# A second mixture of experts whose outputs are scattered to tokens instead of gathered by them

## The chip, the cores and the metric

The kernel runs on one NeuronCore of a Trainium2 chip. The core has a matrix engine (PE), a vector engine (DVE), a scalar engine (ACT), a general engine (POOL, also GpSimd) and a queue engine (SP); each runs its own instruction list in order, and they wait for each other through semaphores. Transfers between memory (DRAM) and the on-chip memory (SBUF) are issued from the SP, ACT or POOL queue and carried out by 16 DMA engines. PE writes its results to PSUM, eight banks that DVE and ACT read. The metric is the device time of one execution, in microseconds (us); less is better.

## The reference

The input is x of 8 sequences of 512 tokens with 128 channels, 4096 tokens in all, in f32. Two layers follow one another, each of the form x + s * silu(g), where s and g are both computed from the normalised x:

```python
xn = layernorm(x)
s = mamba_and_mlp(xn)               # layer 0: a selective scan over 512 steps, then an MLP, two rms norms
g = silu(moe0(xn))                  # 24 experts, top 2 of each token, hidden width 512
x = x + s * g
xn = layernorm(x)
s = attention(xn)                   # layer 1: 8 causal heads
g = silu(moe1(xn))                  # 128 experts, top 2, at most 32 tokens each
x = x + s * g
```

The second mixture (moe1) is where most of the change lies. Each token picks its two best experts, e1 and e2; its place in an expert is the number of earlier tokens that chose it, and second choices come behind all first choices. A choice with a place of 32 or more is dropped:

```python
buf = zeros((E * C, d)).at[idx1].add(xt * v1).at[idx2].add(xt * v2)   # E = 128, C = 32
yb = einsum('ecd,edf->ecf', buf, we)
y = (g1 * v1) * yb[idx1] + (g2 * v2) * yb[idx2]
```

g1 and g2 are the two softmax gates, divided by their sum; v1 and v2 are 1 where the choice was kept.

## The kernel before, in words

**Order.** The Python program is traced into instructions. A planner then orders each engine's list: it starts an instruction when its model says that the inputs and buffers are there, and among ready ones takes the one written earlier. So an instruction can move ahead of others written before it, but once the lists are made, every engine runs its list in order, and one that waits holds all behind it. `follows` and `keep_in_program_order` add edges that fix the order of two instructions of one engine without a wait.

**First layer.** `prepare(b)` normalises a sequence and stores it (`xn_dram`); `places0` and `routing` work out the first mixture's places. `mixture` runs its 24 experts in two passes: `expert1` gathers tokens by POOL's indirect DMAs (L128), multiplies and stores; `between` normalises the hidden rows; `expert2` (L512) gathers them, adds the output bias (L524) and multiplies (L526). The bias is added by a matmul of K = 96 in bf16: the f32 bias is split into three bf16 parts, kept one under another in `bias`, and `chosen(e, r)` picks the three rows of one expert. The recurrent model (`model`, with `front`, `scan`, `back`) is cut into 64 steps that `step()` writes between the experts, and later between the attention heads. Each batch's model result s is stored to `s_dram` (L706).

**Second layer.** `fetch(b)` (L530) loads `o`, `sb` (the stored s) and `xb`, and adds the first mixture's rows to `o` by 8 indirect DMAs (L131). `after` (L545) makes the second layer's input of them: a layernorm, silu, product with `sb` on POOL (L551) and sum (L552). `Attention.prepare` (L752) normalises, finds the top two of 128 experts and the sum of exponentials `se1`, makes the attention's input and calls `route`. `route` (L793) counts places, makes `idx1` (the slot row of each choice, or a spare row beyond the slots) and `row1` (the row of the choice in the output table), and sends each token's row to its slot by 8 scatters per batch (L833), to one table for first choices and one for second choices (`xs_dram[0]`, `xs_dram[1]`). Both tables are zeroed near the start (L272).

Batches 0 to 5 (`EARLY`) run their heads beside the model; batches 6 and 7 run them in the last stage, after the model's end. There, `weights2` (L918) makes the gate weights of all tokens in one pass, and `places` (L930) makes `live`, which is 1 for a slot that may hold a token. `slots(t)` (L956) loads 512 slots of each table and transposes them into `xsT`; `experts(e0)` (L974) multiplies eight experts' slots with their weights into one PSUM bank, DVE multiplies by `live` (L980), and the result is stored to `yb_dram` in one DMA (L981).

`finish(b)` (L983) loads the attention result and the second layer's input of a batch, gathers for each of its four token groups the two rows of `yb_dram` (L993 and L994, through the helper L128, 8 indirect DMAs for each batch), multiplies them by the two weights and adds (L995, L996), takes silu (L997), multiplies by s (L998), adds x (L999) and stores (L1000).

The last stage has 16 heads. They are written with a list of other work: `slots(0)` behind the first head, then 16 experts behind each of the next eight heads, then one `finish` behind each of the next six, and `finish(6)` and `finish(7)` behind the last.

Of the kernel before, what the change touches and what calls it, by code (L numbers as in the profile page):

```python
# [20 lines left out]
P = 128  # L21
# [12 lines left out]
S1 = E1 * C1  # L34
HEADS, DHEAD = 8, 128
# [12 lines left out]
def tile_kernel(ctx: ExitStack, tc: tile.TileContext, t: dict, out: bass.AP):  # L48
# [42 lines left out]

    xs_dram = [dram.tile([S1 + P, D], F32, name=f"xs_dram{k}") for k in range(2)]
    yb_dram = dram.tile([2 * S1, D], F32, name="yb_dram")

# [75 lines left out]
    w121 = w3.tile([P, NTT, 2], F32, name="w121")  # L170
    row1 = w3.tile([P, NTT, 2], I32, name="row1")
    idx1 = w3.tile([P, NTT, 2], I32, name="idx1")
    kp1 = w3.tile([P, NTT, 2], F32, name="kp1")
# [22 lines left out]
    bias = inv_pool.tile([3 * 32, DH + D], BF16, name="bias")  # L196
    zero = inv_pool.tile([P, L], F32, name="zero")
    G.memset(zero, 0.0)
# [72 lines left out]
    for k in range(2):  # L271
        empty = Q.dma_start(  # L272
            xs_dram[k][0:S1, :].rearrange("(p n r) d -> p n (r d)", p=P, r=L // D),
            bc(zero.unsqueeze(1), (P, S1 // L, L)),
        )
        follows(empty, kept)
# [44 lines left out]
    eb = xp.tile([3 * 32, DH + D], F32, name="eb", bufs=1)  # L321
    G.memset(eb, 0.0)
    for k in range(3):
        Q.dma_start(eb[32 * k : 32 * k + E0, 0:DH], t["eb1"])
        Q.dma_start(eb[32 * k : 32 * k + E0, DH:], t["eb2"])
    part = xp.tile([3 * 32, DH + D], BF16, name="part", bufs=1)
# [116 lines left out]
    def expert1(e, w):  # L443
# [10 lines left out]
        for c, r in enumerate(SROWS):  # L454
            ph = ps_e.tile([CP, DH], F32, name="ph", tag="pe")
            T.matmul(ph[:r], chosen(e, r), bias[:, 0:DH], start=True, stop=False)
            T.matmul(ph[:r], xT[:, c * CP : c * CP + r], we, start=False, stop=True)  # L457
            S.activation(hs[:r, c, :], ph[:r], AF.Copy, scale=wsl[:r, c, e : e + 1])
# [53 lines left out]
    def expert2(e, w):  # L512
# [4 lines left out]
        for c, r in enumerate(SROWS):  # L517
# [6 lines left out]
            T.matmul(po[:r, c, :], chosen(e, r), bias[:, DH:], start=True, stop=False)  # L524
            for f in range(NJ):
                T.matmul(po[:r, c, :], hT[:, f, :r], we[:, f, :], start=False, stop=(f == NJ - 1))  # L526
# [3 lines left out]
    def fetch(b):  # L530
# [3 lines left out]
        sb = af.tile([P, NJ, D], F32, name="sb")  # L534
        Q.dma_start(sb, rows(s_dram[b][:, :]))
# [130 lines left out]
    def back(b, yt):  # L666
# [39 lines left out]
        Q.dma_start(rows(s_dram[b][:, :]), xo)  # L706
        yield

# [36 lines left out]
    class Attention:  # L745


        def __init__(self, at, m_qk, w_vo, ps_x, ps_q, ps_s, ps_t, ps_o):
            self.at, self.m_qk, self.w_vo = at, m_qk, w_vo
            self.ps_x, self.ps_q, self.ps_s, self.ps_t, self.ps_o = ps_x, ps_q, ps_s, ps_t, ps_o  # L750

        def prepare(self, b, xb):  # L752

            at, (ps_x, px) = self.at, self.ps_x
            xn2 = at.tile([P, NJ, D], F32, name="xn2", bufs=1)
            layernorm(st, xb, xn2, NJ, eps5, "ln1")
            pt = ps_x.tile([P, L], F32, name="pt2", tag=px)
            for j in range(NJ):
                T.transpose(pt[:, j * P : (j + 1) * P], xn2[:, j, :], ident)
# [15 lines left out]

            sq = at.tile([P, NJ, D], F32, name="sq2", bufs=1)
            ss = st.tile([P, NJ], F32, name="ss2")
            for j in range(NJ):
                S.activation(sq[:, j, :], xn2[:, j, :], AF.Square, accum_out=ss[:, j : j + 1])
# [4 lines left out]
            V.tensor_tensor(sq, xn2, bc(ss.unsqueeze(2), (P, NJ, D)), ALU.mult)  # L784
# [8 lines left out]
        def route(self, b, xn2):  # L793
# [28 lines left out]
            kp = kp1[:, bs, :]  # L822
# [5 lines left out]
            for k in range(2):  # L828
                V.tensor_scalar(pos[:, :, k], pos[:, :, k], float(C1 - 1), float(k * C1), ALU.min, ALU.add)
            V.scalar_tensor_tensor(row1[:, bs, :], e12, float(2 * C1), pos, ALU.mult, ALU.add)  # L830
# [68 lines left out]
        def heads(self, b, xaT):  # L899
# [3 lines left out]
            for hd in range(HEADS):  # L903
# [9 lines left out]
                if hd == HEADS - 1:  # L913
                    Q.dma_start(rows(s1_dram[b][:, :]), s1)
                yield


    def weights2():  # L918
        V.reciprocal(se1, se1)
        V.tensor_tensor(w121, mx1[:, :, 0:2], bc(mx1[:, :, 0:1], (P, NTT, 2)), ALU.subtract)  # L920
        S.activation(w121, w121, AF.Exp)
        V.tensor_tensor(w121, w121, bc(se1.unsqueeze(2), (P, NTT, 2)), ALU.mult)
        den = r3.tile([P, NTT], F32, name="den1")
        V.tensor_tensor(den, w121[:, :, 0], w121[:, :, 1], ALU.add)
        V.tensor_scalar(den, den, EPS32, None, ALU.max)
        V.reciprocal(den, den)
        V.tensor_tensor(w121, w121, bc(den.unsqueeze(2), (P, NTT, 2)), ALU.mult)
        V.tensor_tensor(w121, w121, kp1, ALU.mult)

    def places():  # L930


        pair = r3.tile([P, 2], F32, name="pair")
# [19 lines left out]
        V.tensor_scalar(live, pk, c, float(C1), ALU.add, ALU.is_lt)  # L953


    def slots(t):  # L956
        for k in range(2):
            xg = mo.tile([P, 4, D], F32, name="xg1", bufs=4)
            Q.dma_start(xg, rows(xs_dram[k][t * L : (t + 1) * L, :]))
            px = ps_x.tile([P, 4, P], F32, name="pxs", tag="px")  # L960
            for j in range(4):
                T.transpose(px[:, j, :], xg[:, j, :], ident)
            dst, src = xsT[:, 16 * t : 16 * t + 16, k, :], px.rearrange("p j (e c) -> p (j e) c", c=C1)
            if k == 0:
                V.tensor_copy(dst, src)
            else:
                S.copy(dst, src)

    def load_experts(e0):
        we = mo.tile([P, 8, D], F32, name="we3", bufs=8)  # L970
# [3 lines left out]
    def experts(e0, we):  # L974
        py = ps_x.tile([P, 4, D], F32, name="pye", tag="px")
        for j in range(8):
            h = 2 * C1 * (j % 2)
            T.matmul(py[h : h + 2 * C1, j // 2, :], xsT[:, e0 + j, :, :], we[:, j, :], start=True, stop=True)
        yb = mo.tile([P, 4, D], F32, name="yb", bufs=3)
        V.tensor_tensor(yb, py, bc(live[:, e0 // 2 : e0 // 2 + 4].unsqueeze(2), (P, 4, D)), ALU.mult)  # L980
        Q.dma_start(rows(yb_dram[2 * C1 * e0 : 2 * C1 * (e0 + 8), :]), yb)  # L981

    def finish(b):  # L983
        s1 = mo.tile([P, NJ, D], F32, name="s1f")
# [242 lines left out]
```

## Time and profile before

| | us |
|---|---|
| median of 7 runs | 1570.97 (1561.47 to 1579.28) |
| profiled execution, its own time | 1568.12 |
| its span, from the first to the last instruction | 1566.4 |
| PE busy | 1230.0 |
| DVE busy | 1243.2 |
| ACT busy | 975.7 |
| POOL busy | 619.1 |

| stage (us from the start) | PE busy | DVE busy | POOL busy | DMA share |
|---|---|---|---|---|
| 440 to 640, second pass of the first experts | 172.65 | 142.29 | 92.36 | 0.67 |
| 640 to 710, the second layer begins | 33.89 | 52.51 | 52.97 | 0.40 |
| 750 to 1340, model beside the heads of batches 0 to 5 | 528.15 | 558.78 | 177.11 | 0.24 |
| 1357 to 1566.4, last stage | 164.51 | 126.47 | 72.17 | 0.50 |

The profile is of one execution. Busy time is what an engine spends in its own instructions; idle time stands with what ended it, so "[66.44 <-DMA yb_dram<-yb]" says that the engine was idle for 66.44 us and that the landing of a store to `yb_dram` ended it. "L128" is a line of the kernel; where a helper issues the instruction, it is the helper's line. "SPq" is an instruction that SP issues to its DMA queue. The clock is the share of PE's full clock that was granted. The DMA share is the mean busy share of the 16 DMA engines.

### The profile page before, as it was taken

The numbers are of one execution on the slowest core, as the hardware profiler recorded it, in microseconds if no ns is written. First come the engines' busy times: TensorE is split into PE (matmuls) and PEld (weight loads), VectorE is DVE, ScalarE is ACT, GpSimd is POOL, SyncE is SP. The second block draws the span as 40 slices with busy tenths as digits, with TensorE's granted clock in tenths as the row PEclk, the third lists the DMA queues.
The fourth block names the chain that finished last, engine by engine and source line by source line (L and its number), as shares of the span: only waits on it lengthen the run. The fifth ranks groups of instructions, "written<-read, shape, count | busy, mean of one in ns | idle before, by whom it ended". The sixth has DMA issues, their size and how long they took to land.

```text
span 1566.4 us, 20596 instructions
## 1 busy us (share of the span) xinstructions
PE 1230.0 (79%) x6793; PEld 862.9 (55%) x6793; DVE 1243.2 (79%) x2759; ACT 975.7 (62%) x1726; POOL 619.1 (40%) x504
## 2 busy tenths in 40 slices
PE   6887889513479888647889889989889899898973
PEld 4643445313267776523556656766557567566643
DVE  5629775788966868769999999999989999475564
ACT  5135758666767677455776857767488675563463
POOL 1238743566364444473503651034053301120275
PEclk9769989756599999767989999999989999999987
DMA  6546776787577765523222232124112130249243
GB/s 184 191 149 227 244 238 225 234 273 241 182 243 226 237 193 175 146 60 108 61 75 88 68 103 89 48 74 113 59 34 63 66 102 4 57 127 273 73 125 111
DMA packets 170669, 218.84 MB, mean 140 GB/s; under 512 B 16618, under 2 KB 118074, under 8 KB 170562
## 3 DMA queue, kind: packets, MB, share of 16 engines
q1 hardware_dynamic: 126018, 99.39, 20.6%
q10 hardware_dynamic: 18432, 67.12, 12.8%
q0 software_dynamic: 26112, 51.01, 12.0%
q8 instruction: 54, 0.88, 0.2%
q14 instruction: 53, 0.43, 0.1%
HBM read 161.56 MB, written 55.84 MB: 139 GB/s over the span
## 4 chain that ended last, share of the span: by engine, by line
DVE 38%; PE 30%; DMA 10%; issue 7%; ACT 7%; POOL 7%; SPq 1%; ACTq 0%; POOLq 0%; DVEq 0%
DVE u L610 11%; DVE u L611 5%; PE po L886 4%; PE sc L859 4%; DVE u L608 4%; DVE sc L861 3%; POOL o L131 3%; PE py L632 2%; PE pp L879 2%; PE pqm L851 2%; DMA hd<-hs_dram,row 2%; DMA bb<-xd_dram 2%; DVE s L897 2%; PE po L526 2%; PE ph L457 2%
## 5 line engine op out<-in xcount | busy, mean ns | idle before, releaser
L610 DVE TENSOR_TENSOR_SCAN u<-da,u 128x512 f32<-128x512 f32 x256 | 311.9, 1241 | 51.7 <-ACT da L606 51.6
L632 PE MATMUL py<-ident,u 128*128 128x128 f32 x1024 | 163.8, 301 | 129.9 <-DVE u L611 129.9
L632 PEld LDWEIGHTS py<-ident,u 128*128 128x128 f32 x1024 | 132.1, 155 | 176.5 <-DVE u L611 157.1
L886 PE MATMUL po<-v,pT 128*128 128x129 f32 x1280 | 183.6, 286 | 24.3 <-DVE s L897 15.3
L606 ACT ACTIVATE da<-dt,a_neg 128x512 f32<-128x512 f32 x256 | 176.3, 719 | 38.5 <-DVE u L610 35.1
L886 PEld LDWEIGHTS po<-v,pT 128*128 128x128 f32 x1280 | 165.4, 198 | 54.7 <-issue 24.2
L865 ACT ACTIVATE prob<-sc,mn 128x128 f32<-128x128 f32 (+3 forms) x256 | 130.2, 527 | 97.2 <-DVE mn L861 81.5
L859 PE MATMUL sc<-xaT,qm 128*128 128x128 f32 (+3 forms) x512 | 181.6, 464 | 11.1 <-ACT prob L865 9.0
L608 DVE TENSOR_TENSOR u<-bb,lp 128x1024 f32<-128x1024 f32 x128 | 156.4, 1241 | 13.6 <-DMA bb<-xd_dram 13.6
L611 DVE TENSOR_TENSOR u<-u,cb 128x1024 f32<-128x1024 f32 x128 | 158.0, 1234 | 1.0
L861 DVE CUSTOM_DVE_ANT_0 sc<-sc,mask 128x128 f32<-128x128 f32 (+3 forms) x256 | 125.0, 499 | 29.0 <-PE sc L859 26.9
L131 POOL DMA_INDIRECT o<-os_dram,row x64 | 115.1, 1799 | 76.8 <-DMA bb<-xd_dram 31.9
L128 POOL DMA_INDIRECT xg<-xn_dram,inv x72 | 108.1, 1502 | 85.1 <-PE px L450 37.6
L833 POOL DMA_INDIRECT xs_dram<-xn,idx x64 | 78.1, 1220 | 159.2 <-DVE row L830 73.3
L879 PE MATMUL pp<-ident,prob 128*128 128x128 f32 x640 | 111.9, 284 | 27.1 <-DVE pT L881 22.8
L128 POOL DMA_INDIRECT hg<-hid_dram,inv x72 | 92.7, 1288 | 88.5 <-PE pht L521 60.6
L879 PEld LDWEIGHTS pp<-ident,prob 128*128 128x128 f32 x640 | 79.6, 145 | 85.9 <-issue 34.7
L859 PEld LDWEIGHTS sc<-xaT,qm 128*128 128x128 f32 x512 | 84.9, 200 | 55.2 <-ACT prob L865 25.3
L128 POOL DMA_INDIRECT hd<-hs_dram,row x64 | 81.9, 1280 | 62.3 <-ACT xs L565 23.0
L881 ACT COPY pT<-pp 128x384 f32<-128x384 f32 (+1 forms) x100 | 51.4, 514 | 48.1 <-PE pp L879 47.7
L457 PE MATMUL ph<-we,xTe 128*128 128x512 f32 x144 | 76.2, 660 | 5.7 <-ACT xTe L452 5.7
L526 PE MATMUL po<-we,hgT 128*128 128x128 f32 (+1 forms) x576 | 78.7, 283 | 1.9 <-ACT hgT L523 1.8
(289 smaller groups left out, 2556.3 us busy)
## 6 DMA issues: line engine op xcount, KB each, us to landing
bb<-xd_dram ACTq DMA_DIRECT2D x64, 512.0 KB
cb<-xd_dram ACTq DMA_DIRECT2D x64, 512.0 KB
we<-in_W SPq DMA_DIRECT2D x48, 256.0 KB
hs_dram<-hs SPq DMA_DIRECT2D x24, 512.0 KB
hid_dram<-hd SPq DMA_DIRECT2D x32, 256.0 KB
we<-in_we SPq DMA_DIRECT2D x16, 512.0 KB
hs_dram<-hs SPq DMA_DIRECT2D x24, 192.0 KB
xb<-in_x SPq DMA_DIRECT2D x16, 256.0 KB
```

The lines of the kernel that those rows point to most:

```text
L128: G.indirect_dma_start(dst, None, table[:, :], IOA(idx, 0))
L131: G.indirect_dma_start(dst, None, table[:, :], IOA(idx, 0), compute_op=ALU.add)
L606: S.activation(da[:, j, :], dt[:, hf, :], AF.Exp, scale=a_neg[:, hf, n0 + j : n0 + j + 1])
L608: V.tensor_tensor(u, bb, bc(dx[:, hf : hf + 1, :], (P, NC, L)), ALU.mult)
L610: V.tensor_tensor_scan(u[:, j, :], da[:, j, :], u[:, j, :], 0.0, ALU.mult, ALU.add)
L611: V.tensor_tensor(u, u, cb, ALU.mult)
L632: T.matmul(py[:, i, hf * P : (hf + 1) * P], us[hf][:, j, i * P : (i + 1) * P], ident, is_transpose=True, start=False, stop=(n0 + j == DS - ...
L859: T.matmul(sc[:, :w], qm[:, i * P : w], xaT[:, :w], start=True, stop=True)
L861: V.tensor_tensor_reduce(sc[:, :w], sc[:, :w], mask[:, L - w :], -1.0, FMAX, ALU.add, ALU.min, mn[:, i : i + 1])
L865: S.activation(pr, sc[:, :w], AF.Exp, bias=mn[:, i : i + 1], scale=-1.0)
L879: T.transpose(pp[:, c, :], prob[i][:, k * P : (k + 1) * P], ident)
L886: T.matmul(po[:, i - i0, :], pT[:, i * (i + 1) // 2 + k, :], v[:, k, hd % 4, :], start=(k == 0), stop=(k == i),)
```

## The change

It has these parts:

1. **Slot rows carry more.** A row of the slot tables grows from 128 to 132 floats (`DX`). Behind the token's 128 values stand, for each of the two choices, its weight and its home row, which is the row of the token in `y_dram`. The tables' empty rows get 0 as the weight and -1 as the home row of the table's own choice.
2. **Weights in `prepare`.** `weights2` goes; each `prepare` makes the weights of its batch and puts them and `home` into `xn2`. `row1` and its three operations go.
3. **`places` makes `to`.** Four strided loads on SP fetch weight and home row of every slot from the two tables. `live` becomes the weight for a used slot and 0 for others. `to` is the home row of a used slot, and for an unused one a row of its own beyond the tokens.
4. **Outputs are sent.** `experts` sends the weighted outputs by four scatters of 128 rows for each eight experts to `y_dram`, which has one table for first choices and one for second choices. The 64 scatters are declared free of order among themselves. The token rows of `y_dram` are zeroed by two DMAs on SP behind the first mixture.
5. **`finish` loads rows.** It loads two plain blocks of `y_dram` and adds them. `begin_finish` loads s1 and x1 ahead.
6. **Another order in the last stage.** `slots(0)` stands behind the fifth of the 16 heads, 32 experts behind each of the fifth to the eighth, `begin_finish` of batches 0 to 5 behind the ninth, two `finish` behind each of the last three heads, and batches 6 and 7 at the end. `after(7)` is written ahead of the last stage's pools. `we3` has 6 buffers instead of 8, `yb` 8 instead of 3, and `xsT` is a tile for 16 experts with 3 buffers.
7. **Kept on chip.** The model's last s stays in SBUF (`s_last`), and so do the attention results of batches 6 and 7.
8. **Bias.** The second bias of the first mixture is transposed once into `bias2`, and a transposing matmul of a broadcast column puts it into PSUM; the bf16 parts hold the first bias only.

The diff, cut to its core:

```diff
+DX = D + 4
+EARLY = 6
+NY = NTOK + S1
...
-    xs_dram = [dram.tile([S1 + P, D], F32, name=f"xs_dram{k}") for k in range(2)]
-    yb_dram = dram.tile([2 * S1, D], F32, name="yb_dram")
+    xs_dram = [dram.tile([S1 + P, DX], F32, name=f"xs_dram{k}") for k in range(2)]
+    y_dram = dram.tile([2 * NY, D], F32, name="y_dram")
...
+    empty = inv_pool.tile([P, 2, 2, DX], F32, name="empty")
+    G.memset(empty, 0.0)
+    for k in range(2):
+        G.memset(empty[:, k, :, D + 2 * k + 1 : D + 2 * k + 2], -1.0)
...
-            T.matmul(po[:r, c, :], chosen(e, r), bias[:, DH:], start=True, stop=False)
+
+            T.matmul(
+                po[:r, c, :], bc(bias2[:, e : e + 1], (P, r)), ident, is_transpose=True, start=True, stop=False,
+                skip_group_check=True,
+            )
...
-        Q.dma_start(rows(s_dram[b][:, :]), xo)
+        if b < B - 1:
+            Q.dma_start(rows(s_dram[b][:, :]), xo)
+        else:
+            s_last.append(xo)
...
+            V.reciprocal(se1[:, bs], se1[:, bs])
+            w12 = st.tile([P, NJ, 2], F32, name="w121")
+            V.tensor_tensor(w12, mx1[:, bs, 0:2], bc(mx1[:, bs, 0:1], (P, NJ, 2)), ALU.subtract)
+            S.activation(w12, w12, AF.Exp)
+            V.tensor_tensor(w12, w12, bc(se1[:, bs].unsqueeze(2), (P, NJ, 2)), ALU.mult)
...
+            more = xn2[:, :, D:].rearrange("p j (k a) -> p j k a", a=2)
+            V.tensor_tensor(more[:, :, :, 0], w12, bc(den.unsqueeze(2), (P, NJ, 2)), ALU.mult)
+            V.tensor_copy(more[:, :, :, 1], home[:, bs, :])
...
-            for k in range(2):
-                V.tensor_scalar(pos[:, :, k], pos[:, :, k], float(C1 - 1), float(k * C1), ALU.min, ALU.add)
-            V.scalar_tensor_tensor(row1[:, bs, :], e12, float(2 * C1), pos, ALU.mult, ALU.add)
...
+        more = r3.tile([P, E1 // 2, 2], F32, name="more")
+        for a in range(2):
+            for k in range(2):
+                h = 2 * C1 * a + C1 * k
+                Q.dma_start(
+                    more[h : h + C1], xs_dram[k][0:S1, D + 2 * k : D + 2 * k + 2].rearrange(
+                        "(q a c) d -> a c q d", a=2, c=C1)[a]
+                )
...
+        V.tensor_tensor(live, live, more[:, :, 0], ALU.mult)
...
+        V.scalar_tensor_tensor(own, more[:, :, 1], 0.0, own, ALU.is_lt, ALU.mult)
+        V.scalar_tensor_tensor(to, more[:, :, 1], 0.0, own, ALU.max, ALU.add)
...
-        yb = mo.tile([P, 4, D], F32, name="yb", bufs=3)
+        yb = mo.tile([P, 4, D], F32, name="yb", bufs=8)
         V.tensor_tensor(yb, py, bc(live[:, e0 // 2 : e0 // 2 + 4].unsqueeze(2), (P, 4, D)), ALU.mult)
-        Q.dma_start(rows(yb_dram[2 * C1 * e0 : 2 * C1 * (e0 + 8), :]), yb)
+        for j in range(4):
+            q = e0 // 2 + j
+            sent = G.indirect_dma_start(y_dram[:, :], IOA(to[:, q : q + 1], 0), yb[:, j, :], None)
+            tc.declare_no_dep(sent.ins, group="sent", reason="no two slots have the same row")
+            tc.add_to_no_dep_group("sent", sent.ins)
...
-        y = mo.tile([P, NJ, D], F32, name="y", tag="y")
-        for j in range(NJ):
...
-            gather(ya, yb_dram, row1[:, i, 0:1])
-            gather(yc, yb_dram, row1[:, i, 1:2])
-            V.tensor_scalar(ya, ya, w121[:, i, 0:1], None, ALU.mult)
-            V.scalar_tensor_tensor(y[:, j, :], yc, w121[:, i, 1:2], ya, ALU.mult, ALU.add)
+        y = mo.tile([P, NJ, D], F32, name="y", bufs=3)
+        Q.dma_start(y, rows(y_dram[b * L : (b + 1) * L, :]))
+        y2 = mo.tile([P, NJ, D], F32, name="y2", bufs=3)
+        Q.dma_start(y2, rows(y_dram[NY + b * L : NY + (b + 1) * L, :]))
+        V.tensor_tensor(y, y, y2, ALU.add)
         S.activation(y, y, AF.Silu)
...
+    for k in range(2):
+        tc.keep_in_program_order(
+            Q.dma_start(
+                y_dram[k * NY : k * NY + NTOK, :].rearrange("(p n) d -> p n d", p=P),
+                bc(empty[:, 0, 0:1, 0:D], (P, NTOK // P, D)),
+            )
+        )
     moe.close()
...
+    gate_of = {b: after(b, *fetch(b)) for b in range(EARLY + 1, B)}
     psc.close()
     ssm.close()
...
+    FIRST = 4
+    tokens = {}
+    for i, (b, hd) in enumerate(rest):
+        next(heads[b])
+        if i == FIRST:
+            tokens[0] = slots(0)
+        if FIRST <= i < FIRST + 4:
+            for t16 in (2 * (i - FIRST), 2 * (i - FIRST) + 1):
+                run_experts(t16)
+                if t16 + 1 < E1 // 16:
+                    tokens[t16 + 1] = slots(t16 + 1)
+        if i == FIRST + 4:
+            fetched = {k: begin_finish(k) for k in range(EARLY)}
+        if b == B - 1 and hd >= HEADS - 3:
+            k = 2 * (hd - HEADS + 3)
+            finish(k, *fetched[k])
+            finish(k + 1, *fetched[k + 1])
     for b in range(EARLY, B):
-        finish(b)
+        finish(b, *begin_finish(b))
```

## The prediction

> **What bounds the kernel now.** I read the page's head first, then the waits of the last 90 us, then POOL's order of time there, then a table of stages, and last the chain between the end of the recurrent model and the last attention.
>
> ```profile
> span 1566.4 us, 20596 instructions
> PE 1230.0 (79%) x6793; PEld 862.9 (55%) x6793; DVE 1243.2 (79%) x2759; ACT 975.7 (62%) x1726; POOL 619.1 (40%) x504
> ```
>
> No engine fills the span, so the end is read from its own stage. The waits from 1475 us on:
>
> ```profile
> POOL ya L128 <- DMA yb_dram<-yb: 66.4, 1, 66.4
> DVE ya L995 <- DMA ya<-yb_dram,row: 13.7, 14, 3.4
> DVE y L996 <- DMA yc<-yb_dram,row: 10.4, 13, 2.0
> ```
>
> POOL idles 66.4 us until the last expert output is stored; then it issues all 64 gathers in one train, and DVE, between two heads, waits for them 24 us in all. The train in order of time:
>
> ```profile
> 1476.16 0.98 POOL L128 DMA_INDIRECT ya<-yb_dram,row  x1 [66.44 <-DMA yb_dram<-yb]
> ...
> 1479.18 0.95 POOL L128 DMA_INDIRECT ya<-yb_dram,row  x1 [0.30 <-issue]
> 1480.43 0.94 POOL L128 DMA_INDIRECT yc<-yb_dram,row  x1 [0.30 <-issue]
> ...
> 1557.95 1.01 POOL L128 DMA_INDIRECT yc<-yb_dram,row  x1 [0.30 <-issue]
> ```
>
> One gather each 1.25 us, 83 us from first to last: the train sets the end. The stages (window, us, then busy time of PE, PEld, DVE, ACT, POOL, clock, DMA share, GB/s):
>
> ```profile
> 1357.00:1412.00 55.00, 51.78 (x255) 32.57 (x255) 39.35 (x162) 35.38 (x75) 10.47 (x11) 1.00 0.48 125
> 1412.00:1475.00 63.00, 57.71 (x503) 44.27 (x503) 34.79 (x90) 20.42 (x40) 0.00 (x0) 1.00 0.71 201
> 1475.00:1554.00 79.00, 55.02 (x269) 38.22 (x267) 49.28 (x171) 40.86 (x63) 57.85 (x60) 0.87 0.37 106
> 1554.00:1566.40 12.40, 0.00 (x0) 0.00 (x0) 3.06 (x8) 0.63 (x1) 3.84 (x4) 0.51 0.38 111
> ```
>
> To 1475 PE is busy 93% at full clock; beside the train it falls to 70% at 0.87. The last head ends at 1553.6 (DVE, L897), and 12.8 us of finishing follow. Last, the chain from the model's end:
>
> ```profile
> 1368.72 6.42 DMA sb<-s_dram
> ...
> 1375.29 1.26 POOL o L551
> 1376.63 1.27 POOL xb L552
> ```
>
> The model's last s is ready at 1362.2, but goes to memory, and its load queues on SP behind four expert loads: 13.1 us until L551.
>
> **The change in the last stage.** *Gathers out, scatters in.* 64 gathers leave POOL's tail, 64 scatters come in behind the experts, and `finish` loads plain rows. The nearest price is the first dispatch's scatter (L833): median 0.99 us, starts 1.27 apart where DVE is not crowding. POOL's work is the same; it now runs while POOL was idle.
>
> *PE path.* If nothing holds the heads, PE's remaining work from 1357 is 51.8 + 57.7 + 55.0 x 0.87 = 157.4 us at full clock; at the 93% of the first two windows that takes 169.6, so the heads end at 1526.6 instead of 1553.6. Behind them stand `finish(4)` to `finish(7)`: three 128x512 passes on DVE each, starting 0.61 to 0.71 apart (2 us), then the last store, which took 3.3 us (issued 1563.1, end 1566.4). All four left: 8 + 3.3 + a silu, not over today's 12.8; only the last left: 1.4 + 3.3 = 4.7. I take 9.5, nearer the first, because two of the four are written behind the last head.
>
> *The new read, `more`.* Four loads on SP fetch weight and home row: 32 x 64 pairs of 8 bytes each, 8192 packets, 512 for each of the 16 DMA engines. They wait for the last L833 scatter, the loads of `xg1` queue behind them on SP, and DVE's `live` and `to` wait for them. No row shows it. Below: free but for a landing, 2 us. Above: 256 KB of `xg` landed in 2.69 us alone, 32 packets per engine, 84 ns each: 43 us. Between: in 1420 to 1450, where the DMA engines were full,
>
> ```profile
> 1420.00:1450.00 30.00, 26.67 (x264) 20.94 (x264) 17.42 (x43) 8.88 (x17) 0.00 (x0) 1.00 1.09 306
> ```
>
> a 512 byte packet cost 512 / (306 GB/s / 16) = 27 ns per engine; 512 of them are 14 us, with the landing 16. I take that, since a long run of packets is nearer to a full queue than to a lone load.
>
> The rule that speaks against this read is in the Trainium skill, "DMA: Bandwidth & Descriptors", section "Rules for kernel authors": a last dimension that is not contiguous becomes one descriptor per element, and should be rearranged. The page's floor of about 10.5 ns per packet would, as an estimate, make 5.4 us if it holds for each engine and 86 us if for the whole transfer, and the span by it, early costs included, 1548 or 1612; no row here decides which.
>
> *DVE's wait on it.* In the old order `live` (L953) stood at 1399.5, among the reductions of the third of sixteen heads. If the planner leaves it there, DVE stands up to 18 us (1404 to 1422) and the heads' reductions behind it; if it moves it behind, nothing. I take 5.
>
> *s kept.* L551 need not wait: up to 13.1 us earlier. DVE (9.7 of 10 us from 1380) and PE are full there, so I take 6: the last route's scatters land at 1406 instead of 1412.2. It is worth nothing to the PE path, which is full, and all of it to POOL's.
>
> *Moved on SP.* `after(7)` now stands ahead of the last pools, so its `x1` store can precede the expert loads on SP; these went out from 1364.8 and are first used at 1416: covered by 50 us. The finishes' 12 loads of s1 and x1 go out after the ninth head, 3 MB or 11 us at 300 GB/s, and are used only behind the last scatter: covered by POOL's train.
>
> *POOL path.* `more` lands at 1406 + 16 = 1422; `xg` and the first expert follow 6 us later (xg to first yb took 5.3); 64 x 1.27 = 81.3 brings 1509.3, the last landing 1511.7 (2.4, L833's row). All eight finishes then load 4 MB, 14 us at 300 GB/s, and the last passes and store take 7.3: 1533. That is under the PE path: 1526.6 + 5 + 9.5 = 1541.1. The later of the two decides.
>
> **The rest, all of it cost.** *Bias by a transposed column* (L524): 72 bf16 matmuls of 0.22 become f32 transposes of 0.28 (row L521): 72 x 0.06 = 4.3 on PE, which is 86% busy from 440 to 640. Ends 0 and 4.3; I take 2. *Weights in each `prepare`*: 8 small DVE operations more, 3 less, 8 times; such operations start 0.08 apart and take 0.17. The least is 40 x 0.08 = 3.2, less the old single pass (about 2); the most is 64 x 0.17 = 10.9. DVE is 95% busy from 750 to 1340, so no cover: I take 3. ACT's extra Exp and a table load lie on an engine 69% busy there: nothing, up to 1.3 each if DVE waits. *Zeroing `y_dram`*: 4 MB on SP after the last `os_dram` store (638.5), 8192 packets x 27 ns / 16 = 13.8 us of DMA beside the 16 gathers (L131) which set the chain from 643.9 to 707. SP itself is idle until 688; POOL's issue (1.57 to 1.8 us each) sets that pace, not bytes. Ends 0 and 13.8; I take 2. *Wider slot rows*: the fill at 42.5 us grows by 3%; routing on PE runs over it: 0. GpSimd's shorter bias passes (57 to 66 us) end 30 us before its next work: 0. Sum +7, ends 0 and 29; no gain, as each only adds work.
>
> **Sum.** 1541.1 + 7 = 1548.1 of span, with the 1.7 around it 1549.8, against 1568.1 profiled: -18.3. The median of the runs is 2.9 above the profiled one, so 1571.0 - 18.3 = 1552.7.
>
> **Rivals.**
> *The small read decides (slower).* The POOL path is 111.3 us from `more`'s landing. With the early +7 it ends past 1566.4 once `more` lands after 1448, at 42 us, or 78 ns a packet after its landing time. At 100 ns it is 53 us: 1459 + 118 = 1577, the median 1582. For: the first window's lone load at 84 ns, and tiny rows scattered over 2 MB. Against: the packets of one DMA queue overlap in the full window. 0.17.
> *The early additions eat the gain.* At 20 of their 29, the span is 1561, the median 1566: -0.3%, within the 0.5% that a measurement of this kernel can tell. For: DVE's 95%. Against: 0.08 between small operations. 0.11.
> *Nothing holds the heads and the tail is thin.* 1526.6 + 4.7 + 7 = 1538.3, median 1543. For: today's finishes overlap heads well. Against: the last y loads all wait for the last scatter. 0.20.
> *The finishes hold the last heads.* If the planner puts the first y additions ahead of heads 14 to 16 and the scatters land only at 1520 (1.4 apart, as in crowded rows), three heads of 7.5 and the tail follow: 1520 + 3 + 22.5 + 9.5 + 7 = 1562, but heads written before take part of it: 1555, median 1560, -0.7%. 0.12.
>
> **How the numbers follow.** The forecast has 0.40; its own range is 1543 to 1564. Forecast, thin tail and held heads are over 0.5% faster, 0.72; the eaten gain is the same, 0.11; the small read is slower, 0.17. The range goes from 1534 (the thin tail without early costs, 1531.3 + 1.7 + 2.9 = 1536, and a little) to 1582, the small read at 100 ns.
>
> **What would show it.** POOL busy with scatters from about 1428 to 1510 and idle after; no wait of DVE for gathers; PE at 90% or more to the last head; `more` landing within 20 us of the last L833. Wrong would be: DVE or PE idle for tens of us on `more` near 1410 to 1450, POOL's scatters 1.6 us apart, or a DVE stage from 750 to 1340 that is over 15 us longer.

## The result, and the profile after

The changed kernel is slower: 1586.29 us (median of 19 runs, 1577.42 to 1598.42) against 1568.61 us (46 runs of the kernel before, 1554.18 to 1579.28). The ratio is 1.0115, 95% interval 1.0098 to 1.0131. Forecast were 1552.7 us and "faster". The profiled execution took 1576.40 us (span 1574.7); it lies 9.9 us under its median, and just under the lowest of the 19 runs; that of before lies 0.5 under its own median.

Lines of the changed kernel are a little lower in the file: the slot scatters are L868 (L833 before), the first gather's helper is L132 (L128), the output scatters are L1031, the loads of y L1047 and L1049, the addition of the two y tiles L1050, silu L1051, the products and sums L1052 and L1053, a head's first and later sums L930 and L932, the model's last addition L723 (L704).

The page of the changed kernel begins:

```profile
span 1574.7 us, 20528 instructions
PE 1215.6 (77%) x6794; PEld 856.2 (54%) x6794; DVE 1225.7 (78%) x2732; ACT 981.0 (62%) x1742; POOL 603.8 (38%) x511
```

PE, DVE and POOL have each a little less to do than before, and still the span is longer: time is lost to waiting. The waits of the changed kernel from 1475 us on (engine and what it stood at, what it waited for, us in total, times, longest):

```profile
DVE y L1050 <- DMA y<-y_dram: 34.2, 3, 32.6
PEld po L921 <- issue: 33.3, 4, 32.6
PE po L921 <- DVE s L930: 32.4, 1, 32.4
ACT y L1051 <- DVE y L1050: 31.2, 1, 31.2
```

The 66.4 us in which POOL waited for the last expert output are gone, and so are the 24 us of DVE at the gathered rows. In their place stands one wait of 32.6 us, and it holds three engines: DVE at the first y addition, ACT at the silu behind it, and PE at a matmul that needs a buffer which DVE has yet to empty. DVE's order there:

```profile
1477.51 0.70 DVE L896 CUSTOM_DVE_ANT_0 sc<-sc,mask 128x512 f32<-128x512 f32 x1 [0.57 <-PE sc L894]
1478.13 0.14 DVE L896 DVE_READ_ACCUMULATOR2_ANT mn<- 128x1 f32 x1
1510.91 0.69 DVE L1050 TENSOR_TENSOR y<-y,y 128x512 f32<-128x512 f32 x1 [32.65 <-DMA y<-y_dram]
1511.52 0.16 DVE L926 RECIPROCAL rsum<-po 128x2 f32<-128x2 f32 x1
1511.60 0.28 DVE L896 CUSTOM_DVE_ANT_0 sc<-sc,mask 128x128 f32<-128x128 f32 x1
1511.80 0.14 DVE L896 DVE_READ_ACCUMULATOR2_ANT mn<- 128x1 f32 x1
1511.80 0.61 DVE L930 TENSOR_SCALAR s<-po,rsum 128x128 f32<-128x128 f32 x2
```

L930 is the first head of a batch. So `finish(0)`'s addition, which is written behind the 14th of the 16 heads, stands in DVE's list ahead of the sums of the ninth. Its rows are complete only when the last of the 64 scatters has landed. POOL's scatters and the load behind them, in order of time:

```profile
1424.61 0.97 POOL L1031 DMA_INDIRECT y_dram<-yb,to  x1 [6.47 <-DMA xg<-xs_dram]
1425.89 0.97 POOL L1031 DMA_INDIRECT y_dram<-yb,to  x1 [0.31 <-issue]
```

The chain that ended last goes from the train through the addition to the heads (start, us, what):

```profile
1504.86 2.23 DMA y_dram<-yb,to
...
1507.52 3.30 DMA y<-y_dram
1512.55 3.26 PE po L921 x14
```

The stages of the changed kernel (window, us; busy time of PE, PEld, DVE, ACT, POOL; clock, DMA share, GB/s):

```profile
1358.00:1478.00 120.00, 110.86 (x735) 76.50 (x736) 72.16 (x240) 56.47 (x116) 51.80 (x57) 0.96 0.63 163
1478.00:1511.00 33.00, 2.14 (x11) 1.08 (x9) 0.35 (x3) 2.46 (x4) 21.32 (x22) 0.60 0.21 68
1511.00:1569.00 58.00, 49.23 (x280) 37.74 (x280) 42.84 (x129) 41.04 (x60) 0.00 (x0) 0.93 0.36 101
1569.00:1574.70 5.70, 0.00 (x0) 0.00 (x0) 2.16 (x5) 0.00 (x0) 0.00 (x0) 0.90 0.17 46
```

For 33 us hardly anything but POOL works; half of the last stage's heads come after. From the model's last addition (1356.36 before, 1357.85 after) to the end of the span it took 210.0 us before and takes 216.9. The forecast had 184.7 for it (1541.1 - 1356.4). 216.9 - 32.65 = 184.2: in this profile the stand alone is as large as the difference. That it fits so closely is in part luck, as the kernel without the stand shows below (187.6 us).

The rule for this is in the Trainium skill, "TensorE: Matmul & The Clock Gate", section "Architectural detail: the array is 16× 32×32, not 1× 128×128": the queues of ACT and DVE are strictly first in, first out, and on PE only weight loads are pulled ahead. The trace agrees: in the 32.65 us nothing behind L1050 ran on DVE.

### The profile page after: what moved, and what is told of

It is laid out like the page before. It is cut to its first block, busy times and chain, and to the rows that moved or that the text cites. A ratio compares the mean times of both kernels' runs of the same rounds, so it can differ in the third digit from the quotient of the medians.

```text
span 1574.7 us, 20528 instructions
## 1 busy us (share of the span) xinstructions
PE 1215.6 (77%) x6794; PEld 856.2 (54%) x6794; DVE 1225.7 (78%) x2732; ACT 981.0 (62%) x1742; POOL 603.8 (38%) x511
## 4 chain that ended last, share of the span: by engine, by line
DVE 36%; PE 29%; DMA 9%; issue 9%; POOL 8%; ACT 8%; SPq 1%; POOLq 0%; ACTq 0%; DVEq 0%
DVE u L629 11%; DVE u L630 5%; PE po L921 5%; PE sc L894 4%; DVE u L627 4%; DVE sc L896 3%; PE pp L914 2%; POOL o L135 2%; PE py L651 2%; POOL y_dram L1031 2%; PE po L542 2%; DMA bb<-xd_dram 2%; DVE s L932 2%; PE ph L469 2%; DMA hd<-hs_dram,row 1%
## 5 line engine op out<-in xcount | busy, mean ns | idle before, releaser
L629 DVE TENSOR_TENSOR_SCAN u<-da,u 128x512 f32<-128x512 f32 x256 | 306.6, 1221 | 40.8 <-ACT da L625 40.7
L921 PEld LDWEIGHTS po<-v,pT 128*128 128x128 f32 x1280 | 168.8, 200 | 84.2 <-issue 47.0
L625 ACT ACTIVATE da<-dt,a_neg 128x512 f32<-128x512 f32 x256 | 175.6, 718 | 31.4 <-DVE u L629 29.9
L132 POOL DMA_INDIRECT xg<-xn_dram,inv x72 | 107.7, 1495 | 107.6 <-PE px L462 46.1
L868 POOL DMA_INDIRECT xs_dram<-xn,idx x64 | 80.7, 1262 | 166.8 <-DVE idx L865 68.0
L914 PEld LDWEIGHTS pp<-ident,prob 128*128 128x128 f32 x640 | 80.1, 145 | 86.6 <-issue 32.6
L132 POOL DMA_INDIRECT hg<-hid_dram,inv x72 | 86.9, 1207 | 89.6 <-PE pht L533 63.4
L132 POOL DMA_INDIRECT hd<-hs_dram,row x64 | 76.4, 1194 | 67.4 <-ACT xs L584 23.3
```

The source lines that it names most:

```text
L132: G.indirect_dma_start(dst, None, table[:, :], IOA(idx, 0))
L625: S.activation(da[:, j, :], dt[:, hf, :], AF.Exp, scale=a_neg[:, hf, n0 + j : n0 + j + 1])
L629: V.tensor_tensor_scan(u[:, j, :], da[:, j, :], u[:, j, :], 0.0, ALU.mult, ALU.add)
L914: T.transpose(pp[:, c, :], prob[i][:, k * P : (k + 1) * P], ident)
L921: T.matmul(po[:, i - i0, :], pT[:, i * (i + 1) // 2 + k, :], v[:, k, hd % 4, :], start=(k == 0), stop=(k == i),)
```

## The experiments

The theory (W in short): the loss is the place of the first y addition in DVE's list. The rival: the scatters or the small read `more` load POOL or the DMA engines so much that the last stage is slower whatever the order (L). Ratios are to the kernel before, run beside each group on its chip. Because single executions differ by some 15 us ahead of the last stage, profiles are compared from the model's last addition to the end of the span, "last stage" in the table at the end of this section.

**The addition pinned (e1_pin).** The one line that stood too early keeps its written place:

```diff
-        V.tensor_tensor(y, y, y2, ALU.add)
+        tc.keep_in_program_order(V.tensor_tensor(y, y, y2, ALU.add))
```

> The addition of the two y blocks in finish is held behind the head it is written after (an edge on DVE, no wait); nothing else differs from the changed kernel. Theory W: the loss is DVE standing 32.6 us at the first of these additions, seven heads early, for the end of the scatter train, with PE idle beside it. Then DVE has no stand of over 5 us between 1450 and the end, the train still ends near 1506, the last head near 1538, and the span is 25 to 33 us under the changed kernel's 1574.7: a ratio to the kernel before of 0.990 to 0.996. Rival L: the loss is the load that the scatters and the small read put on the DMA engines and POOL; then the stand only moves elsewhere and the ratio stays over 1.005.

Measured: 1559.28 us, ratio 0.9907 (0.9874 to 0.9941). The same four kinds of window in the pinned kernel:

```profile
1365.00:1478.00 113.00, 103.14 (x714) 72.23 (x714) 69.16 (x231) 53.00 (x108) 48.05 (x54) 0.98 0.66 171
1478.00:1511.00 33.00, 32.99 (x186) 23.36 (x186) 19.10 (x70) 19.20 (x40) 25.05 (x26) 1.00 0.16 53
1511.00:1535.00 24.00, 19.69 (x128) 15.26 (x126) 17.48 (x52) 15.36 (x25) 0.00 (x0) 1.00 0.58 165
1535.00:1552.80 17.80, 0.00 (x0) 0.00 (x0) 10.03 (x17) 2.52 (x4) 0.00 (x0) 0.62 0.59 167
```

PE, idle for 31 of the 33 us from 1478 in the changed kernel, works through them here while POOL scatters as ever (26 scatters in the window). The last stage falls from 216.9 to 187.6 us. The ordering edges of one line, which `finish` writes eight times, turn 1.2% slower into 0.9% faster; no instruction does other work. That is what W says, and it leaves L nothing of the last stage's loss to explain.

**Half of the scatters (e5_half).** Every second scatter is left out of the changed kernel.

```diff
-        for j in range(4):
+        for j in range(0, 4, 2):
```

> The changed kernel with every second scatter left out (half of the second mixture's outputs are not sent), DVE's order as there. W: the train ends near 1424 + 41 = 1466, before DVE reaches the first addition at 1478, so the stand is gone with the order unchanged: span near 1542, ratio 0.988 to 0.996. If the stand had another cause, such as the loads of y themselves or SP's queue, it stays and the ratio is over 1.005.

Measured: 1565.34 us, ratio 0.9948 (0.9916 to 0.9979). Here the rows of y are nearly there when DVE reaches the early addition:

```profile
1494.35 0.69 DVE L1050 TENSOR_TENSOR y<-y,y 128x512 f32<-128x512 f32 x1 [2.66 <-DMA y<-y_dram]
1497.60 0.69 DVE L1050 TENSOR_TENSOR y<-y,y 128x512 f32<-128x512 f32 x1 [2.02 <-DMA y<-y_dram]
```

The last stage takes 188.2 us, the pinned kernel's 187.6. With half of the scatters the two early additions wait 4.7 us; with all of them the first alone waits 32.65. Nor do 32 fewer scatters bring anything that the pin does not: the scatters themselves are covered.

**The addition on POOL, without a pin (p1_pool_free).** The changed kernel, with one letter changed:

```diff
-        V.tensor_tensor(y, y, y2, ALU.add)
+        G.tensor_tensor(y, y, y2, ALU.add)
```

> The changed kernel with the addition on POOL and no pin. DVE has no instruction left that waits for a scatter directly, but ACT's first silu stands at the same place of ACT's order as in the changed kernel (among the exponentials of the ninth or tenth head), and waits for the addition. If the loss is the order of an engine that the heads need, ACT takes DVE's place: ACT stands 25 to 35 us, PE idles 20 to 30 beside it, ratio 1.005 to 1.012. If the loss is of DVE alone, the stand goes and it is the pinned kernel's 0.991.

Measured: 1587.99 us, ratio 1.0124 (1.0079 to 1.0170). ACT's order of time in it:

```profile
1485.34 0.96 ACT L900 ACTIVATE prob<-sc,mn 128x512 f32<-128x512 f32 x2
1486.32 1.28 ACT L1051 ACT_TABLE_LOAD   x1
1519.05 0.63 ACT L1051 ACTIVATE y<-y 128x512 f32<-128x512 f32 x1 [31.45 <-POOL y L1050]
```

ACT now stands 31.45 us at the silu, ahead of the exponentials that the heads need, and PE is busy 10.2 of the 35 us from 1480 to 1515. So the loss is not DVE's alone: it comes back when another engine that the heads need does the waiting. In the changed kernel itself ACT stands at the same silu, 31.2 us, beside DVE.

**All finishes behind the last head (e2_last)**, pinned; the eight `finish` are written after the loop:

```diff
-        if b == B - 1 and hd >= HEADS - 3:
-            k = 2 * (hd - HEADS + 3)
-            finish(k, *fetched[k])
-            finish(k + 1, *fetched[k + 1])
+    for k in range(EARLY):
+        finish(k, *fetched[k])
```

> As e1_pin, with all eight finishes behind the last head. W: no stand either, heads end some 5 us earlier as DVE does nothing else, but eight finishes of 2 us on DVE and the last store follow, 18 to 22 us: ratio 0.993 to 0.999, between e1_pin and the kernel before. L: over 1.005.

Measured: 1572.56 us, ratio 0.9992 (0.9965 to 1.0019). No wait holds the heads, but nothing covers the finishes: 29 us with PE idle stand behind the last head.

```profile
1542.00:1571.00 29.00, 0.44 (x4) 0.25 (x3) 16.93 (x27) 5.15 (x9) 0.00 (x0) 0.59 0.63 181
```

So the place of the finishes is worth as much as the rest of the change, which takes 22.4 us off the last stage (210.0 to 187.6): too early costs 29 us of it, too late 11.

**Finishes among four heads (e4_pin4)**, pinned; two behind each of heads 13, 14 and 15, the seventh behind the last, the eighth after all.

```diff
-        if b == B - 1 and hd >= HEADS - 3:
-            k = 2 * (hd - HEADS + 3)
+        if b == B - 1 and hd >= HEADS - 4:
+            k = 2 * (hd - HEADS + 4)
...
```

> As e1_pin, but two finishes behind each of heads 13, 14 and 15, the seventh behind the last, and only the eighth after all heads. W: the train ends near 1506 and head 13 near 1514, so the additions find their rows there; the tail behind the last head shrinks by some 4 to 8 us against e1_pin, ratio 0.985 to 0.993. If the rows come later than head 13, DVE stands a few us and it is no better than e1_pin. L: over 1.005.

Measured: 1562.52 us, ratio 0.9935 (0.9904 to 0.9965), last stage 188.0 us. Not better than e1_pin: the heads end later by what the end gets shorter. The last PE instruction ends 175.6 us behind the model's end (169.7 in e1_pin), and 12.4 us before the end of the span (17.9).

**Pins behind the head, and more buffers (b1_head, b3_headbufs).** In e1_pin each addition also has to follow the finish before it, and so waits for its silu. Here it follows only its head's last DVE instruction; b3_headbufs has five buffers for y and y2 as well.

```diff
-                        V.scalar_tensor_tensor(so, po[:, i - i0, 0:D], r, so, ALU.mult, ALU.add)
+                        self.done = V.scalar_tensor_tensor(so, po[:, i - i0, 0:D], r, so, ALU.mult, ALU.add)
...
-        V.tensor_tensor(y, y, y2, ALU.add)
+        follows(V.tensor_tensor(y, y, y2, ALU.add), last.done)
```

> As the pinned kernel (0.9907), but the first addition of each finish has to stand behind the last DVE instruction of the attention head that it is written behind, no longer behind the finish before it. If the pinned kernel's tail came from the finishes waiting for each other through ACT's silu (0.70 us, six times, in its rows), the last store comes about 4 us earlier: ratio 0.988, about 1555 us, behind the last PE instruction 14 us or less. If it came from the loads of y, which wait for one of three buffers (1.11 us wait, and a load of 4.41 us behind a store in its chain), the time stays at 0.991.

> As the one before, with five buffers for y and for y2 instead of three. If the loads of the last finishes wait for a store to free a buffer, 1542.19 to 1546.63 leaves the pinned kernel's chain: another 4 us, ratio 0.985, 1550 us, with the last PE instruction followed by 6 to 9 us. If DVE's own work is the limit of the tail (eight finishes of three passes of 0.6 us, 15 us), it stays where the one before is.

Measured: 1564.47 us, 0.9932 (0.9901 to 0.9963), and 1558.34 us, 0.9893 (0.9860 to 0.9926). The head's pin alone gains nothing over e1_pin. The buffers gain about 4 per mille over the pin alone, as expected of them, though the intervals of the two overlap; the last stage is 192.5 and 188.0 us. What follows the last PE instruction falls from 17.2 to 13.2 us: by the 4 us expected, but not to the 6 to 9. Against e1_pin, b3_headbufs is not distinguishable.

**The addition on POOL, pinned (c1_pool, c2_pool4).** b3_headbufs with the addition on POOL; c2_pool4 with finishes among four heads as well.

```diff
-        follows(V.tensor_tensor(y, y, y2, ALU.add), last.done)
+        follows(G.tensor_tensor(y, y, y2, ALU.add), last.done)
```

> Head pins and five buffers, and the addition of the two y tiles goes from DVE to POOL, which has nothing behind its scatters; it still has to stand behind the last DVE instruction of its head. If DVE's passes are the limit of the tail (12 us of 0.6 us passes in a row in the kernel with five buffers), a third of them leaves DVE: 2 to 4 us less, ratio 0.987. A POOL addition of 128x512 is an estimate of 1.1 us from 1.39 us for 96x640, eight of them in a row 9 us: if these become the limit instead, it stays at 0.989.

> As the one before, with two finishes behind each of the heads 13, 14 and 15, the seventh behind head 16 and only the eighth after all heads. If the finishes behind the last head are the tail, the tail of 13 us falls to about 8: ratio 0.984 to 0.986. If the heads get later by what the tail loses, as with four heads in the pinned kernel (last head 4 us later, relative to the last route), it is the same as the one before.

Measured: 1562.35 us, 0.9925 (0.9888 to 0.9962), and 1562.89 us, 0.9939 (0.9908 to 0.9969). Neither gains. A POOL addition takes 1.27 us, DVE's 0.69, and POOL waits 23.4 us for loads of y in c1_pool. That points to the loads and away from the passes; that the slower addition ate a small gain is not excluded.

**The old bias (u1_bias)**, on e1_pin: both biases of the first mixture in bf16 parts again.

```diff
-            T.matmul(
-                po[:r, c, :], bc(bias2[:, e : e + 1], (P, r)), ident, is_transpose=True, start=True, stop=False,
-                skip_group_check=True,
-            )
+            T.matmul(po[:r, c, :], chosen(e, r), bias[:, DH:], start=True, stop=False)
...
```

> The pinned kernel with the old bias (both biases of the first mixture in one tile of three bf16 parts, second one added through chosen rows). If the f32 transpose is what the expert passes pay, the time from the first expert gather to the last matmul of the second passes falls by 3 to 4.5 us, to 541 (540.4 before, 544.8 after). If the shorter loads of the biases are what brought the first gather from 96.6 to 87.6, it goes back to 95 to 97, and the total is 4 to 6 us above the pinned kernel's 0.9907; if that gain is of another part of the change, it stays at 85 to 93 and the total is 4 below.

Measured: 1567.96 us, ratio 0.9962 (0.9937 to 0.9986). The first gather is back at 97.97 us (96.59 before; 84.6 to 93.1 in the twelve profiles with the new bias), and the passes behind it take 542.7 us (540.4 before; 544.8 to 560.1 with the new bias). So both go with the new bias: within this group the first gather comes about 13 us earlier and the passes take about 11 us longer, and the second passes end where they ended, at 640.7 us against 638.0 to 640.1 in the three others of this group. Whether the passes are longer because of the transposes, or because they begin earlier and their end is set by other work, was not separated. By the total, undoing it brings no gain.

**The last s through memory (u2_s)**, on e1_pin:

```diff
-        if b < B - 1:
-            Q.dma_start(rows(s_dram[b][:, :]), xo)
-        else:
-            s_last.append(xo)
+        Q.dma_start(rows(s_dram[b][:, :]), xo)
...
```

> The pinned kernel with the last s through memory again. From the model's last addition to the last route's first scatter: 30.9 us in the pinned kernel, 33.6 after, 43.3 before; back to 41 to 44 if keeping s is what shortened it. Total: if the scatters and what follows set the end, 8 to 10 us more than the pinned kernel (0.996 to 0.997); if PE's heads set it, as I reckoned, 0 to 3 us more (0.991 to 0.993), since in the pinned kernel the last scatter lands 10 us ahead of the first y addition.

Measured: 1561.47 us, ratio 0.9912 (0.9881 to 0.9942). From the model's last addition to the last route's first scatter it takes 39.0 us, 30.9 in e1_pin: 2 less than expected, but most of the way back. Yet the first output scatter comes 66.1 us behind the model's end, as in the kernels that keep s (64.3 in e1_pin, 66.7 to 68.4 in the others but d1_more2), and the last stage takes 185.8 against 187.6. Keeping s brings the route 8 us forward and the end not at all.

**The small read twice (d1_more2)**, on e1_pin: each of the four loads of `more` issued twice.

```diff
+                for _ in range(2):
...
```

> The pinned kernel with each of the four small reads issued twice: 16384 packets of 8 bytes instead of 8192. From the first issue to the landing it was 6.9 us, 4.0 behind the last issue. If the packets set it, as I reckoned with 27 ns for each packet of an engine (14 us), it becomes 11 to 14 us; if the issue on SP sets it (3.94 us for four), 10 to 11. In both cases the total stays at the pinned kernel's 0.991 within 0.3%, as the first scatter follows the landing by 16 us; if the small read is on the way to the end, 4 to 7 us more, 0.994 to 0.996.

Measured: 1568.37 us, ratio 0.9980 (0.9947 to 1.0013). Against the pinned kernel's 0.9907, measured on another chip, that is 11 us more, and the intervals are apart. Against c1_pool and c2_pool4 on its own chip it is 6 to 9 us more, and the intervals overlap. DVE stands longer for the read, here in d1_more2:

```profile
1430.62 0.23 DVE L990 TENSOR_TENSOR live<-live,more 128x64 f32<-128x64 f32 x1 [7.36 <-DMA more<-xs_dram]
```

In e1_pin the same wait (L989) is 3.93 us. PE is held with it: a wait for ACT's exponentials, which wait for DVE, grows from 3.8 to 5.9 us. The first output scatter comes 70.4 us behind the model's end, 64.3 to 68.4 in the others, and the last stage takes 193.8 us, 187.6 in e1_pin and 191.0 in u1_bias, where the read is single. So 3.4 us more of DVE's standing are shown, and with them a second, small case of the same kind: an early instruction that waits for a transfer, in a list that the heads need. That the read is on the way to the end is likely; how much of the 11 us is its own, and how much the spread of profiles and chips, stays open. What packets and what SP's issue have of it stays open: the second four went out 4.86 us long and behind an `xg` load, and landed 7.6 us after their first issue.

The stages of each kernel, us, from one profile each. "passes" is from the first expert gather to the last matmul of the second passes, "between" from there to the second layer's first slot scatter, "model" from there to the model's last addition:

| kernel | first gather | passes | between | model | last stage | ratio |
|---|---|---|---|---|---|---|
| before | 96.6 | 540.4 | 96.0 | 623.4 | 210.0 | 1 |
| after | 87.6 | 544.8 | 98.1 | 627.4 | 216.9 | 1.0115 |
| p1_pool_free | 87.5 | 549.3 | 100.5 | 627.3 | 214.7 | 1.0124 |
| e2_last | 84.7 | 560.1 | 98.2 | 629.4 | 198.5 | 0.9992 |
| d1_more2 | 92.5 | 550.5 | 101.3 | 628.8 | 193.8 | 0.9980 |
| u1_bias | 98.0 | 542.7 | 97.9 | 632.0 | 191.0 | 0.9962 |
| e5_half | 93.1 | 551.5 | 101.2 | 627.9 | 188.2 | 0.9948 |
| c2_pool4 | 85.1 | 553.9 | 101.3 | 629.3 | 189.4 | 0.9939 |
| e4_pin4 | 87.8 | 553.2 | 100.7 | 630.0 | 188.0 | 0.9935 |
| b1_head | 84.6 | 555.5 | 101.6 | 628.3 | 192.5 | 0.9932 |
| c1_pool | 87.6 | 556.9 | 101.6 | 628.6 | 187.7 | 0.9925 |
| u2_s | 85.1 | 553.2 | 98.3 | 629.5 | 185.8 | 0.9912 |
| e1_pin | 87.5 | 552.6 | 100.9 | 624.2 | 187.6 | 0.9907 |
| b3_headbufs | 84.8 | 553.2 | 100.8 | 620.9 | 188.0 | 0.9893 |

By their intervals, both e1_pin and b3_headbufs are faster than the kernel before and the changed one.

## Why the prediction was wrong

**The bound of before** was read rightly: with POOL's late train gone and nothing in its place, the last stage falls from 210.0 to 187.6 us (e1_pin).

**The step that failed** is the condition under which the PE path was summed: "If nothing holds the heads". The forecast put the finishes where they are written, behind heads 14 to 16, and charged only the wait for `more` (5 us). The planner's own freedom to move an instruction ahead was used for `more` and for one rival, "The finishes hold the last heads", but not for this sum. That rival is what happened, with the right mechanism and a wrong place: it had the additions ahead of heads 14 to 16, with the scatters late at 1520. They stood ahead of the ninth, with the scatters on time at 1507. Held there, eight heads instead of three come after the train, and 32.65 us are lost where the rival found room for a small gain. Why the planner thought the rows ready so early was not examined.

**Terms of the last stage, without the stand.** The sum was 184.7 us, e1_pin measures 187.6. That it is so near is in part luck, as two errors cancel. By the forecast's own mark, a head's last sum on DVE (L932), the heads of e1_pin end 171.6 us behind the model's end, where 1526.6 and a wait of 5 gave 175.2; and the tail behind them is 16.0 us instead of 9.5, over the upper bound of 12.8. The tail was priced by DVE passes in a row, but loads of y that wait for buffers, silus and stores lie between them. In e1_pin's chain a store ends, the load that needs its buffer follows, and DVE waits for it:

```profile
1539.56 2.55 DMA out<-y
1542.14 0.05 issue
1542.19 4.41 DMA y<-y_dram
1546.63 0.70 DVE y L1050
```

In the changed kernel, where the last y addition starts at 1547.1, 23 us before the heads end, the tail is 4.9 us, at the thin end.

**POOL's train** came as reckoned: 1.27 us a scatter, 1424.6 to 1505.8 and landed at 1507.1 (forecast 1428 to 1509.3 and 1511.7).

**`more`** landed 6.9 us after its first issue (1401.63 to 1408.50) instead of 16, so the slower rival fell. A full queue's 27 ns for a 512 byte packet was the wrong neighbour for packets of 8 bytes: 512 for each engine in 6.9 us are at most 13.4 ns each. The estimate of 5.4 us from the Trainium skill, "DMA: Bandwidth & Descriptors", section "Bandwidth", with its 10.5 ns a packet taken per engine, is nearer, and the 86 us for the whole transfer are excluded. The rule quoted beside it, on a last dimension that is not contiguous, does not quite meet this read: its last dimension is a contiguous pair, and the trace has one packet of 8 bytes for each of the 8192 pairs. DVE's wait on the read was forecast at 5 and measured 3.47.

**s kept** was forecast at 6 us for POOL's path and none for PE's. The route came 8.2 us earlier (L868 at 1391.43, L833 at 1399.64), but within the spread of the profiles nothing of this reaches the first output scatter (u2_s). That PE's own order of heads decides when the slots are transposed would fit; no run shows it. For the end it is worth nothing, as forecast.

**The early costs**, forecast at +7 with bounds 0 and 29. In the two profiles the model ends only 1.5 us later, but the changed kernel's profile is 9.9 us under its median. By the medians the rest of the kernel costs 17.7 - 6.9 = 10.8 us; for e1_pin it is -13.4 + 22.4 = +9.0. The size was about right, the parts were not. The bias was forecast at 2, at most 4.3 and never a gain: with it the first gather comes 3 to 12 us earlier and the passes take 4 to 20 longer. "Model" was forecast at 3 and is 4 to 9 us longer in all profiles but two, "between" at 2 and is 2 to 6. With one profile of before, how the 10.8 divides stays open.

## What to carry to other kernels

When a planner orders an in-order engine, an instruction that waits for a late transfer has to be priced where the planner may put it, and not where it is written. The worst case is the time from its earliest place to the landing, and it holds every engine that needs what stands behind it in the same list. An ordering edge without a wait is enough to hold it in place. A waiting instruction that is given to another engine stays as costly if the next one in the chain has the same early place. Moving work away from the end of a critical path gains only what the place of its consumers lets through: too early cost 29 us here, too late 11.

## What the hardware showed that was not expected

**PE's clock near the start.** Windows of before, and then of after (columns as in the stages above; the clock is the third from the right):

```profile
32.00:50.00 18.00, 17.52 (x90) 10.16 (x89) 11.07 (x61) 11.16 (x18) 0.00 (x0) 1.00 0.66 224
50.00:62.00 12.00, 12.00 (x70) 7.60 (x70) 6.33 (x15) 0.00 (x0) 4.76 (x6) 0.60 0.86 253
62.00:68.00 6.00, 1.55 (x11) 1.36 (x9) 6.00 (x12) 0.00 (x0) 3.54 (x3) 0.78 0.00 0
68.00:92.00 24.00, 23.03 (x131) 19.73 (x131) 6.08 (x11) 5.48 (x7) 0.00 (x0) 0.50 0.32 99
```

```profile
32.00:50.00 18.00, 10.98 (x75) 9.50 (x75) 11.19 (x57) 6.85 (x13) 5.90 (x8) 1.00 0.79 261
50.00:62.00 12.00, 8.92 (x57) 5.88 (x56) 6.27 (x18) 0.44 (x2) 0.00 (x0) 1.00 0.90 247
62.00:68.00 6.00, 2.62 (x8) 1.51 (x8) 4.31 (x10) 0.03 (x1) 0.00 (x0) 1.00 0.01 3
68.00:92.00 24.00, 24.00 (x157) 17.10 (x156) 6.67 (x17) 2.89 (x4) 3.53 (x4) 1.00 0.24 71
```

Before, PE is busy almost without a gap from 32 to 62 us, and its clock falls to 0.50 by 54 us, in the middle of that work. It then idles 5.4 us and works on at 0.50 to 92. After, with gaps from 32 on and 6.5 us of idling from 58.9, it keeps the full clock. The old bias brings the low clock back (u1_bias: 0.50 from 70 to 92; the twelve profiles with the new bias have 1.00 from 68 to 92), so it goes with this part of the change; what in it decides was not tried. The low clock and the late first gather (96.6 and 98.0 us, 84.6 to 93.1 with the new bias) come together; that one makes the other was not tried either. In the Trainium skill, "TensorE: Matmul & The Clock Gate", section "What's actually happening", it is idleness that halves the clock; here the clock fell while PE was busy, and held through a longer idle time, so the page's rule alone does not explain these rows.

**Tiny packets were cheap.** 8192 packets of 8 bytes, strided over rows of 528 bytes, landed 6.9 us after the first of four issues, 3.9 us of which were SP's issuing.
